# Turning the gates and the squares behind the quadrants of a decoder kernel, with another order of work in its first and last heads

## The chip, the cores and the metric

The kernel runs on one core of a Trainium2 chip. The metric is the device time of one execution in microseconds (us). Before the change the median of three runs is 1415.98 us, between 1415.79 and 1416.11.

## The reference, cut to what matters

The input is x, 16 sequences of 256 tokens with 512 features. Three blocks follow one another, each with a residual and a layer norm behind it: a gated state-space block, a long convolution that takes the place of cross attention, and a feed-forward block with low-rank experts. The change lies in the last two:

```python
# long convolution: D = 256 tokens are 32 heads x 8, L = 512
kv = vr[:, :, :, None, :] * x2r[:, :, None, :, :]
y = irfft(rfft(kv, n=1024) * k_f[None, :, None, None, :], n=1024)[..., :L]
y = y + kv * skip
out = jnp.einsum('bhijl,bhil->bhjl', y, x1r)
x = _layernorm(x + out)
# feed-forward with the two best of eight low-rank experts
base = x_flat @ W.T + b
logits = x_flat @ gate_w.T + gate_b
topk_logits, topk_idx = jax.lax.top_k(logits, 2)
gates = jax.nn.softmax(topk_logits, axis=-1)
xA = jnp.einsum('nd,erd->ner', x_flat, lora_A)
delta_all = jnp.einsum('ner,eor->neo', xA, lora_B)
...
out = base + lora_update
x = _layernorm(x + out)
```

## The kernel before, in words

All numbers are float32. Stage one (to about 760 us) is the state-space block; the change leaves it alone but for one constant. Stage two is one Python loop over the heads, `for h in range(HX)`, HX = 32; a head has 128 tokens (16 sequences by 8). The order of instructions on each engine is the order of the program, written out by hand (`manual_schedule`), so an instruction that waits holds up all that stands behind it on its engine.

Pass h of the loop convolves head h and does the feed-forward of head f = h - 1. It has two halves, one for each half q of the sequences.

- First half: four transposes turn v of the next head (`turned_v`, L147, tile `tr`); parts of earlier feed-forwards follow; then `turned_gates` (L1222) transposes `xa`, the gated low-rank activations of the head before, and ScalarE copies it to `xaT` (L1224). `seeded` (L1012) makes the seed product of the convolution, `spread_seed` lets ScalarE copy it into the other PSUM banks (L1019), and `convolve` makes four full products (L1030) and twelve 64x64 quadrant products (L1045). The last four quadrants wait for `one`, a tiny ScalarE copy (L1061) that itself waits for the first four.
- Second half: directly behind the quadrants `products_with_gates` multiplies the head's output `o_l` by the gate and low-rank weights `w_gl` (L1198: 8 gate columns, 128 low-rank columns and one column of 1/512 for the mean), and multiplies the squares `sq` by a column of 1/512 (L1202) for the mean square. Then come parts of the feed-forward, the seed and the convolution for q = 1.

A float32 product appears as two matmul records, a transpose as one.

VectorE contracts the convolution's result with the context: two products `pr` that read the PSUM banks of y (L1078) and two reductions `red` (L1088). It also makes the products `kv` of the next head (L157), and `gates` (L1119 to L1150), the ranking of the eight experts. GpSimd sums `ol` (L1402), folds the squares from 512 to 128 columns (L1190), takes the power -1/2 for the layer norm, and prepares `xs`, `Td` and `sk`. ScalarE makes the squares (L1186) and the mean squared (`m2`, L1207).

The feed-forwards of heads 1 to 30 go in pairs (`class Pair`), a seven-product scheme over 2x2 blocks with the products `first`, `second`, `third_and_fifth`, `sixth`, `fourth` and `seventh`, dealt over two passes. A pair begins in the second half of an odd pass (3, 5 and so on) with `first` and `third_and_fifth`. The even pass behind it makes `sixth` and `second` in its first half, and `fourth`, the first low-rank product and `finish` of the pair's first head in its second. `seventh`, the second low-rank product and the other `finish` (L1156, VectorE) follow in the first half of the next odd pass. All of a pair lies in two PSUM banks, `al` and `be`. Head 0 is alone: four plain products of 512 columns (`feed_forward`, L1238) and one low-rank product (`lora`) into one bank, `base`. Two of the four are made in pass 1, two and the low-rank product in pass 2. Head 31 is finished behind the loop, among the last full products of its own convolution: `convolve(..., True, steps=...)` calls one step ahead of each of them.

PSUM tiles of the tag `tr` (two buffers) hold `tr` and `gl` in turn; `gl` has the products of L1198 and L1202, then serves VectorE as scratch for the ranking (`room`), and takes the turned gates in its last 128 columns (`XAT`). The lines around the change:

```python
            if nxt:
                seed = seeded(y, T, xs, 1, h == 0)
            if ff:
                if f == 0:
                    feed_forward(base, o_l, (1,))
                    alone = base, o_l, rs
                elif second:
                    pair.third_and_fifth()
...
                turning = gates(gl, rs, gl[:, NG + 2 :]), gl[:, XAT]
            if nxt:
                convolve(y, kv, T, Td, 1)
```

Of the kernel before, what the change touches and what calls it, by code (L numbers as in the profile page):

```python
# [72 lines left out]
def decoder_kernel(  # L73
# [108 lines left out]
    with ExitStack() as s1:  # L182
# [370 lines left out]
        for g in range(groups):  # L553
# [339 lines left out]
            if g == 0:  # L893
                skip_bc = wp.tile([P, S], F32, name="skip_bc")
                nc.sync.dma_start(skip_bc, skip.partition_broadcast(P))
                w_gl = wp.tile([P, KD, NG + 1], F32, name="w_gl")
                nc.gpsimd.memset(w_gl[:, :, NG:], 1.0 / D)
# [12 lines left out]
                share = wp.tile([P, P], F32, name="share")  # L910
                nc.gpsimd.memset(share, 1.0 / D)
# [4 lines left out]
    with ExitStack() as s2:  # L916
# [197 lines left out]
            nc.gpsimd.tensor_tensor(rs, var, nhalf[:, 0:1], ALU.pow)  # L1114
            return nm, rs

        def gates(gl, rs, room):


            seen, rank = [room[:, 2 * NE * NE + n * NE :][:, 0:NE] for n in range(2)]  # L1120
            lg = p2.tile([P, NE], F32, tag="lg", name="lg")
            for to in (seen, lg):
# [27 lines left out]
            return xa  # L1150
# [40 lines left out]

            return sq[:, 0:P], folded

        def products_with_gates(o_l, sq):

            gl = ps_t.tile([P, D], F32, tag="tr", name="gl")
            for kc in range(KD):
                nc.tensor.matmul(  # L1198
                    gl[:, 0 : NG + 1], o_l[:, kc, :], w_gl[:, kc, :],
                    start=(kc == 0), stop=(kc == KD - 1),  # L1200
                )
            last = nc.tensor.matmul(  # L1202
                gl[:, NG + 1 : NG + 2], sq, share[:, 0:1],
                start=True, stop=True, skip_group_check=True,
            )
# [4 lines left out]
        def spread_of(gl, m2):  # L1210

            var = p2.tile([P, 1], F32, tag="var_b", name="var_b")
            nc.vector.scalar_tensor_tensor(
                var, gl[:, NG + 1 : NG + 2], LN_EPS, m2, ALU.add, ALU.subtract
            )
            rs = p2.tile([P, 1], F32, tag="rs_h", name="rs_h", bufs=4)
            nc.gpsimd.tensor_tensor(rs, var, nhalf[:, 0:1], ALU.pow)
            return rs

        def turned_gates(xa, room):  # L1220
            xat = room[0:ER, 0:P]
            nc.tensor.transpose(xat, xa.rearrange("p e r -> p (e r)"), ident)  # L1222
            xaT = p2.tile([ER, P], F32, tag="xaT", name="xaT")
            nc.scalar.copy(xaT, xat)  # L1224
            return xaT

        HD = D // 2
        LO, HI, ALL = slice(0, HD), slice(HD, D), slice(0, D)
        XAT = slice(D - P, D)

        def lora(ps, xaT, cols, start=False):
            nc.tensor.matmul(  # L1232
# [123 lines left out]
        last, alone, turning = None, None, None  # L1356
        pair, closing, ready = None, None, None
        for h in range(HX):
            nxt, ff, f = h + 1 < HX, last is not None, h - 1
# [8 lines left out]
            if h:  # L1368
# [4 lines left out]
                        vns.append(load_v(h + 2))  # L1373
                        cTs.append(load_c(h + 2))
                opened = pair if pair is not None and len(pair.o) == 2 else None
                if alone is not None:
                    feed_forward(alone[0], alone[1], (2, 3))
                if opened is not None:
                    opened.sixth()
                if closing is not None:  # L1380
                    closing.seventh()
                xaT = turned_gates(*turning) if turning is not None else None
                if pair is not None:
                    pair.xaT.append(xaT)
# [5 lines left out]
                if alone is not None:  # L1390
# [7 lines left out]
            if ff:  # L1398
# [7 lines left out]
                    ALU.add,  # L1406
                )
                sq, folded = squares(o_l)
                if alone is not None:
                    base, _, rs_f = alone  # L1410
                    ready = finish(0, ((ALL, base, b_bc),), rs_f, folded)
                    alone = None
# [36 lines left out]
            y = new_y()  # L1449
            o = with_residual(skip_term(cT, ws, behind), vT)  # L1450
            if ff:
                gl, m2 = products_with_gates(o_l, sq)
                if second:
                    pair.first()
                if closing is not None:
                    closing.fourth()
                    closing.scaled_first()
                if not nxt:
                    pair.sixth()
                rs = spread_of(gl, m2)  # L1460
                if second and nxt:
                    pair.sums_second()
                if f == 0:
                    base = ps_b.tile([P, D], F32, tag="al", name="base")
                    feed_forward(base, o_l, (0,), True)
            if nxt:
                seed = seeded(y, T, xs, 1, h == 0)
            if ff:
                if f == 0:
                    feed_forward(base, o_l, (1,))  # L1470
                    alone = base, o_l, rs
# [20 lines left out]
            if ff:  # L1492
                if second and nxt:
                    pair.sums_third()
                if not nxt:
                    pair.common()
                turning = gates(gl, rs, gl[:, NG + 2 :]), gl[:, XAT]
            if nxt:
                convolve(y, kv, T, Td, 1)
                if closing is not None:  # L1500
# [6 lines left out]


        o_f, red_f, y_f, cT_f = last
        o_l = {}  # L1510

        def contracted(src, ks):

# [42 lines left out]
            )  # L1556

        def turn():
            pair.xaT.append(turned_gates(*turning))
# [11 lines left out]
        convolve(  # L1571
            y_f, kv, T, Td, 1, True, steps=(pair.second, turn, pair.lora_of_first, rest)
        )
        tr = ps_t.tile([P, KD, P], F32, tag="tr", name="tr")
        base = ps_y.tile([P, 2, D], F32, tag="y0", name="y0")[:, 0, :]
# [94 lines left out]
```

## Time and profile before

| what | value |
|---|---|
| median of three runs | 1415.98 us |
| the profiled execution, its own time | 1415.68 us |
| its span, first to last instruction | 1413.9 us |
| TensorE (PE) matmul busy | 1397.6 us, 99% |
| VectorE (DVE) busy | 1179.5 us, 83% |
| GpSimd (POOL) busy | 612.4 us, 43% |
| ScalarE (ACT) busy | 422.3 us, 30% |
| mean granted clock of TensorE | 0.998 |

PE is the row of matmuls, PEld that of weight loads, which mostly run beside matmuls. Each matmul's record lasts longer than its turn in the array: what counts for the time is the distance from one start to the next. A row of a timeline has its start, its length, the engine, the line, the operation, and in brackets the idle time before it with what ended that. The chain of waits names the work that followed on itself without a gap and ended last.

### The profile page before, as it was taken

Reading aid. Unit: us, or ns where it says so; the run is one execution under the profiler, and the core shown is the slowest. Engines: PE = TensorE matmul, PEld = TensorE weight load, DVE = VectorE, ACT = ScalarE, POOL = GpSimd, SP = SyncE. Lnnn points to the kernel's source line nnn. Section 1 sums busy time; section 2 is a strip of 40 time slices with the busy share of each in tenths; the row PEclk is TensorE's granted clock in tenths of the full one; section 3 lists DMA queues with packets and bytes.
Section 4 is the critical chain, followed back from the end, with each engine's and each line's share of the span. In section 5 each row is a group of like instructions: output and inputs, shape, how many; then the busy total and the mean of one; then the engine's idle time right before and its main releaser. Section 6 shows DMA issues by size and latency. Waiting matters only on the chain.

```text
span 1413.9 us, 19593 instructions
## 1 busy us (share of the span) xinstructions
PE 1397.6 (99%) x7122; PEld 953.6 (67%) x7122; DVE 1179.5 (83%) x2270; ACT 422.3 (30%) x917; POOL 612.4 (43%) x816
## 2 busy tenths in 40 slices
PE   9999999999999999999999999999999999999997
PEld 7888888787888888878885355454545555555543
DVE  6988878878888787877857888898989888889886
ACT  2423323233232332332311323332323233333321
POOL 5450011110100201001005677788777777788774
PEclk9999999999999999999999999999999999999999
DMA  8013111120121111203003112221222122212200
GB/s 303 33 38 133 34 58 45 38 84 8 52 71 45 56 36 39 84 22 92 31 8 115 58 40 75 76 69 51 75 68 67 48 73 75 75 53 68 68 27 30
DMA packets 49168, 89.20 MB, mean 63 GB/s; under 512 B 8880, under 2 KB 13360, under 8 KB 49072
## 3 DMA queue, kind: packets, MB, share of 16 engines
q1 hardware_dynamic: 49072, 87.96, 19.6%
q8 instruction: 56, 0.92, 0.3%
q14 instruction: 40, 0.33, 0.1%
HBM read 70.62 MB, written 17.32 MB: 62 GB/s over the span
## 4 chain that ended last, share of the span: by engine, by line
PE 95%; DVE 2%; POOL 2%; issue 1%; DMA 0%; ACT 0%; SPq 0%; POOLq 0%; DVEq 0%
PE mm L330 21%; PE y L1030 15%; PE s L330 14%; PE y L1045 12%; PE s L782 6%; PE mm L782 6%; PE y L1012 4%; PE be L1260 4%; PE al L1260 3%; PE gl L1198 2%; PE tr L147 1%; PE xm L599 1%; PE mm L739 1%; PE mm L873 1%; PE al L1232 1%; PE s L873 1%
## 5 line engine op out<-in xcount | busy, mean ns | idle before, releaser
L1078 DVE TENSOR_TENSOR pr<-y,cT 128x1024 f32<-128x1024 f32 x126 | 148.4, 1219 | 59.1 <-PE y L1045 59.1
L1045 PE MATMUL y<-kv 64*64 64x512 f32 x1536 | 179.8, 598 | 0.6 <-ACT one L1061 0.6
L588 DVE SCALAR_TENSOR_TENSOR acc<-xi,wc,acc 128x512 f32<-128x512 f32 x192 | 142.0, 753 | 7.4 <-ACT acc L584 1.7
L1088 DVE TENSOR_REDUCE red<-pr 128x128 f32<-128x1024 f32 x126 | 147.1, 1209 | 0.0
L157 DVE TENSOR_TENSOR kv<-tr,cT 128x1024 f32<-128x1024 f32 x124 | 145.5, 1215 | 0.0
L1045 PEld LDWEIGHTS y<-kv 64*64 64x64 f32 x1536 | 52.2, 132 | 119.5 <-issue 96.6
L1030 PE MATMUL y<-kv 128*128 128x512 f32 x272 | 128.9, 595 | 2.0 <-DVE pr L1078 1.7
L68 POOL TENSOR_TENSOR rs_a<-ve_a,nhalf 128x1 f32<-128x1 f32 x32 | 19.0, 592 | 242.5 <-DVE ve_a L66 242.5
L391 POOL TENSOR_TENSOR rstd<-ms,nhalf 128x4 f32<-128x4 f32 (+1 forms) x9 | 8.5, 948 | 251.4 <-DVE ms L389 251.4
L1030 PE MATMUL y<-kv,Td 128*128 128x512 f32 x248 | 116.5, 592 | 0.0
L330 PE MATMUL mm<-XT,w_z 128*128 128x256 f32 x384 | 90.7, 379 | 0.0
L1030 PEld LDWEIGHTS y<-kv,Td 128*128 128x128 f32 x248 | 47.2, 190 | 59.2 <-issue 55.7
L1030 PEld LDWEIGHTS y<-kv 128*128 128x128 f32 x272 | 50.9, 190 | 43.6 <-ACT y L1019 18.5
L996 POOL TENSOR_TENSOR xs<-kv 128x512 f32<-128x512 f32 x63 | 80.2, 1272 | 0.1
L1019 ACT COPY y<-y 64x512 f32<-64x512 f32 x120 | 67.0, 558 | 44.2 <-PE y L1012 41.9
L330 PEld LDWEIGHTS mm<-XT,w_z 128*128 128x128 f32 x384 | 73.1, 190 | 9.8
L330 PE MATMUL mm<-xnT,w_z 128*128 128x256 f32 x288 | 70.8, 382 | 0.0
L1402 POOL TENSOR_TENSOR ol<-o,red 128x512 f32<-128x512 f32 x31 | 39.3, 1269 | 69.7 <-DVE red L1088 69.7
L223 POOL TENSOR_TENSOR XT<-xnT 128x512 f32<-128x512 f32 x7 | 9.2, 1310 | 129.0 <-PE mm L782 129.0
L1012 PE MATMUL y<-xs,kv 128*128 128x512 f32 x120 | 62.8, 605 | 0.8 <-POOL xs L996 0.7
L330 PE MATMUL s<-XT,w_xi 128*128 128x256 f32 x256 | 61.0, 380 | 0.8 <-DVE XT L226 0.5
L330 PEld LDWEIGHTS mm<-xnT,w_z 128*128 128x128 f32 x288 | 54.1, 190 | 10.0 <-issue 3.0
(326 smaller groups left out, 3053.6 us busy)
## 6 DMA issues: line engine op xcount, KB each, us to landing
cT<-in_ctxT SPq DMA_DIRECT2D x32, 384.0 KB
kv<-in_toep SPq DMA_DIRECT2D x32, 384.0 KB
xt<-in_x SPq DMA_DIRECT2D x32, 256.0 KB
spread<-both SPq DMA_DIRECT2D x32, 256.0 KB
first<-xt SPq DMA_DIRECT2D x32, 256.0 KB
vn<-first SPq DMA_DIRECT2D x32, 256.0 KB
out<-res SPq DMA_DIRECT2D x31, 256.0 KB
xnT<-in_xT SPq DMA_DIRECT2D x7, 1024.0 KB
```

The costliest lines, as they stand in the source:

```text
L157: last = nc.vector.tensor_tensor(kv[:, q, k * BQ : (k + NL // 2) * BQ], vT[:, q, blks].rearrange("p k (b i) -> p (k b) i", i=NH).unsqueeze ...
L330: nc.tensor.matmul(ps, w[:, p, a, kc, :], Xs[b][:, kc, :], start=start and kc == 0, stop=stop and kc == 1, skip_group_check=upon,)
L588: ins = nc.vector.scalar_tensor_tensor(acc, xi[:, :, k : k + S], wc[:, c, k : k + 1], acc, ALU.mult, ALU.add)
L782: nc.tensor.matmul(ps, own[a][c][:, n * P : (n + 1) * P], w_o[b][c], start=start and c == 0, stop=stop and c == HC - 1, skip_group_check=upon,
L996: return nc.gpsimd.tensor_tensor(xs[:, q], moving(kv, q, 0), moving(kv, q, 1), ALU.add)
L1012: nc.tensor.matmul(seed, T[:, SHARED_AT, :], xs[:, q], start=True, stop=True)
L1019: nc.scalar.copy(bank_of(y, 2)[b : b + HP], seed[a : a + HP])
L1030: nc.tensor.matmul(bank_of(y, lb), w, moving(kv, q, mb), start=not late and lb not in begun, stop=False, skip_group_check=True,)
L1045: return nc.tensor.matmul(bank_of(y, lb)[cols], T[rows, DIAGONAL_AT, (b - a) * HP : (b - a + 1) * HP], moving(kv, q, lb)[rows], start=star ...
L1078: nc.vector.tensor_tensor(pr.rearrange("p (k b j) i -> p k b j i", k=2, j=NH), y[i].rearrange("p k (b j i) -> p k b j i", j=NH, i=NH), cT[ ...
L1088: nc.vector.tensor_reduce(red[:, q, 2 * i : 2 * i + 2, :].rearrange("p k t -> p (k t)"), pr, AX.X, ALU.add)
L1260: nc.tensor.matmul(ps, a[:, kc, :], w[:, kc, :], start=(start and kc == 0), stop=(kc == 1), skip_group_check=True,)
```

## The change

- `products_with_gates` begins with two transposes directly behind the quadrants: that of `xa` of the head before (taken out of the first half, so it runs half a pass later), and that of `sq`. The product of `sq` by the column of 1/512 goes. `w_gl` gets one column more, of -1/512, so mean squared is the product of two of its columns.
- ScalarE sums the turned squares by an activation with `accum_out` (128x128 out of PSUM) in place of squaring the mean (128x1), and copies the turned gates (`turned_copy`) in the second half.
- Head 0's feed-forward: product 0 in pass 1 behind the seed, 1 and 2 in the first half of pass 2, 3 in its second half, the low-rank product and `finish` in pass 3.
- Last head: `sixth` behind `third_and_fifth`; the finishing of head 29 (`first_finished`) one step ahead of `seventh` and the second low-rank product, with a full product between them; the ranking of the very last head has its scratch in SBUF, and one scaled copy of the logits less.

```diff
-        def products_with_gates(o_l, sq):
+        def products_with_gates(o_l, sq, xa):
             gl = ps_t.tile([P, D], F32, tag="tr", name="gl")
+            if xa is not None:
+                nc.tensor.transpose(gl[0:ER, XAT], xa.rearrange("p e r -> p (e r)"), ident)
+            turned = gl[:, NG + 2 : NG + 2 + P]
+            nc.tensor.transpose(turned, sq, ident)
             for kc in range(KD):
                 nc.tensor.matmul(
-                    gl[:, 0 : NG + 1], o_l[:, kc, :], w_gl[:, kc, :],
-                    start=(kc == 0), stop=(kc == KD - 1),
+                    gl[:, 0 : NG + 2], o_l[:, kc, :], w_gl[:, kc, :],
+                    start=(kc == 0), stop=(kc == KD - 1), skip_group_check=True,
                 )
-            last = nc.tensor.matmul(
-                gl[:, NG + 1 : NG + 2], sq, share[:, 0:1],
-                start=True, stop=True, skip_group_check=True,
-            )
-            m2 = p2.tile([P, 1], F32, tag="m2", name="m2")
-            wait_for(nc.scalar.activation(m2, gl[:, NG : NG + 1], AF.Square), last)
-            return gl, m2
+            ms = p2.tile([P, 1], F32, tag="ms", name="ms")
+            nc.scalar.activation(
+                sq, turned, AF.Identity, bias=eps, scale=1.0 / D, accum_out=ms
+            )
+            return gl, ms
...
+        def turned_copy(room):
+            xaT = p2.tile([ER, P], F32, tag="xaT", name="xaT")
+            nc.scalar.copy(xaT, room[0:ER, 0:P])
+            return xaT
...
                 var, gl[:, NG + 1 : NG + 2], LN_EPS, m2, ALU.add, ALU.subtract    # before
+                var, gl[:, NG : NG + 1], gl[:, NG + 1 : NG + 2], ms, ALU.mult, ALU.add
...
-                if alone is not None:
-                    feed_forward(alone[0], alone[1], (2, 3))
+                if h == 2:
+                    feed_forward(base, alone, (1,))
+                if h == 3:
+                    lora(base, xaT, ALL)
...
-                xaT = turned_gates(*turning) if turning is not None else None
                 seed = seeded(y, T, xs, 0, h == 1)
...
-                    lora(alone[0], xaT, ALL)
+                if h == 2:
+                    feed_forward(base, alone, (2,))
...
-                gl, m2 = products_with_gates(o_l, sq)
+                gl, ms = products_with_gates(o_l, sq, xa)
+                if xa is not None:
+                    xaT = turned_copy(gl[:, XAT])
...
-                if not nxt:
-                    pair.sixth()
...
-                    feed_forward(base, o_l, (1,))
+                    feed_forward(base, o_l, (0,), True)
                 elif second:
                     pair.third_and_fifth()
+                    if not nxt:
+                        pair.sixth()
                 else:
                     pair = Pair(f, o_l)
+                if f == 1:
+                    feed_forward(base, alone, (3,))
...
-        def rest():
-            ready.append(pair.finish(0))
+        def first_finished():
+            ready.append(pair.finish(0))
+        def rest():
             pair.seventh()
             pair.lora_of_second()
...
-        xaT = turned_gates(gates(gl, rs, gl[:, NG:]), gl[:, XAT])
+        xaT = turned_gates(gates(gl, rs), gl[:, XAT])
```

More of the change, by code (lines that the diff above doesn't have):

```diff
@@ L895, in decoder_kernel @@
                 nc.sync.dma_start(skip_bc, skip.partition_broadcast(P))
-                w_gl = wp.tile([P, KD, NG + 1], F32, name="w_gl")
-                nc.gpsimd.memset(w_gl[:, :, NG:], 1.0 / D)
+                w_gl = wp.tile([P, KD, NG + 2], F32, name="w_gl")
+                for n, part in enumerate((1.0 / D, -1.0 / D)):
+                    nc.gpsimd.memset(w_gl[:, :, NG + n : NG + n + 1], part)
                 nc.sync.dma_start(w_gl[:, :, 0:NG], WglT.rearrange("(k p) e -> p k e", p=P))
@@ L1115, in centred_squares, with gates @@
             return nm, rs
-        def gates(gl, rs, room):
-            seen, rank = [room[:, 2 * NE * NE + n * NE :][:, 0:NE] for n in range(2)]
+        def gates(gl, rs, room=None):
             lg = p2.tile([P, NE], F32, tag="lg", name="lg")
-            for to in (seen, lg):
+            if room is None:
+                room = p2.tile([P, 2 * NE * NE + NE], F32, tag="cmp", name="cmp", bufs=1)
+                rank, seen = room[:, 2 * NE * NE :], lg
+            else:
+                seen, rank = [room[:, 2 * NE * NE + n * NE :][:, 0:NE] for n in range(2)]
+            for to in (lg,) if seen is lg else (seen, lg):
                 nc.vector.scalar_tensor_tensor(to, gl[:, 0:NE], rs, gb_bc, ALU.mult, ALU.add)
@@ L1192, in squares, with spread_of @@
             return sq[:, 0:P], folded
[L1194 removed]
+        HD = D // 2
+        LO, HI, ALL = slice(0, HD), slice(HD, D), slice(0, D)
+        XAT = slice(D - P, D)
+        eps = w2.tile([P, 1], F32, name="eps")
+        nc.gpsimd.memset(eps, LN_EPS / P)
+        def products_with_gates(o_l, sq, xa):
             gl = ps_t.tile([P, D], F32, tag="tr", name="gl")
+            if xa is not None:
+                nc.tensor.transpose(gl[0:ER, XAT], xa.rearrange("p e r -> p (e r)"), ident)
+            turned = gl[:, NG + 2 : NG + 2 + P]
+            nc.tensor.transpose(turned, sq, ident)
             for kc in range(KD):
                 nc.tensor.matmul(
[L1199 to L1210 removed]
+                    gl[:, 0 : NG + 2], o_l[:, kc, :], w_gl[:, kc, :],
+                    start=(kc == 0), stop=(kc == KD - 1), skip_group_check=True,
+                )
+            ms = p2.tile([P, 1], F32, tag="ms", name="ms")
+            nc.scalar.activation(
+                sq, turned, AF.Identity, bias=eps, scale=1.0 / D, accum_out=ms
+            )
+            return gl, ms
[3 more added lines that the diff above has]
+            return xaT
+        def spread_of(gl, ms):
             var = p2.tile([P, 1], F32, tag="var_b", name="var_b")
             nc.vector.scalar_tensor_tensor(
[L1214 removed]
+                var, gl[:, NG : NG + 1], gl[:, NG + 1 : NG + 2], ms, ALU.mult, ALU.add
             )
@@ L1220, in turned_gates @@
         def turned_gates(xa, room):
[L1221 to L1229, printed above, removed]
+            nc.tensor.transpose(room[0:ER, 0:P], xa.rearrange("p e r -> p (e r)"), ident)
+            return turned_copy(room)
         def lora(ps, xaT, cols, start=False):
@@ L1354, in finish @@
                 return finish(self.f + head, self.parts(head), self.rs[head], between)
-        last, alone, turning = None, None, None
+        last, xa = None, None
         pair, closing, ready = None, None, None
@@ L1381, in decoder_kernel @@
                     closing.seventh()
-                xaT = turned_gates(*turning) if turning is not None else None
-                if pair is not None:
-                    pair.xaT.append(xaT)
                 seed = seeded(y, T, xs, 0, h == 1)
@@ L1389, in decoder_kernel @@
                     ready = None
-                if alone is not None:
-                    lora(alone[0], xaT, ALL)
+                if h == 2:
+                    feed_forward(base, alone, (2,))
                 if opened is not None:
@@ L1408, in decoder_kernel @@
                 sq, folded = squares(o_l)
[L1409 to L1412, printed above, removed]
+                if h == 3:
+                    ready = finish(0, ((ALL, base, b_bc),), rs_alone, folded)
                 elif closing is not None:
@@ L1451, in decoder_kernel @@
             if ff:
-                gl, m2 = products_with_gates(o_l, sq)
+                gl, ms = products_with_gates(o_l, sq, xa)
+                if xa is not None:
+                    xaT = turned_copy(gl[:, XAT])
+                    for one in (pair, closing):
+                        if one is not None and one.f <= f - 1 <= one.f + 1:
+                            one.xaT.append(xaT)
                 if second:
@@ L1457, in decoder_kernel @@
                     closing.scaled_first()
[L1458 to L1460 removed]
+                rs = spread_of(gl, ms)
                 if second and nxt:
                     pair.sums_second()
[L1463 to L1465 removed]
             if nxt:
@@ L1469, in decoder_kernel @@
                 if f == 0:
-                    feed_forward(base, o_l, (1,))
-                    alone = base, o_l, rs
+                    base = ps_b.tile([P, D], F32, tag="al", name="base")
+                    feed_forward(base, o_l, (0,), True)
+                    alone, rs_alone = o_l, rs
                 elif second:
                     pair.third_and_fifth()
+                    if not nxt:
+                        pair.sixth()
                 else:
                     pair = Pair(f, o_l)
+                if f == 1:
+                    feed_forward(base, alone, (3,))
                 if f:
@@ L1496, in decoder_kernel @@
                     pair.common()
-                turning = gates(gl, rs, gl[:, NG + 2 :]), gl[:, XAT]
+                xa = gates(gl, rs, gl[:, NG + 2 :])
             if nxt:
@@ L1509, in decoder_kernel @@
         o_f, red_f, y_f, cT_f = last
-        o_l = {}
+        gl_f, o_l = gl, {}
         def contracted(src, ks):
@@ L1558, in turn @@
         def turn():
-            pair.xaT.append(turned_gates(*turning))
+            pair.xaT.append(turned_gates(xa, gl_f[:, XAT]))
             pair.fourth()
@@ L1571, in decoder_kernel @@
         convolve(
-            y_f, kv, T, Td, 1, True, steps=(pair.second, turn, pair.lora_of_first, rest)
+            y_f, kv, T, Td, 1, True,
+            steps=(pair.second, turn, pair.lora_of_first, first_finished, rest),
         )
```

## The prediction

> **What bounds the kernel now.** I read the page's engine and chain rows, then the chain over two passes in mid-loop, then each place where TensorE's queue is held: its weight loads against VectorE's timeline, the early passes, the last one.
>
> ```profile
> PE 1397.6 (99%) x7122; PEld 953.6 (67%) x7122; DVE 1179.5 (83%) x2270; ACT 422.3 (30%) x917; POOL 612.4 (43%) x816
> PE 95%; DVE 2%; POOL 2%; issue 1%; DMA 0%; ACT 0%; SPq 0%; POOLq 0%; DVEq 0%
> ```
> ```profile
> 1019.95 0.11 PE gl L1202 x2
> 1020.06 0.97 PE al L1260 x4
> ...
> 1029.79 0.59 PE tr L147 x4
> 1030.37 0.87 PE al L1260 x4
> ```
> ```profile
> 1030.86 0.14 PEld L1222 LDWEIGHTS gl<-ident,xa 128*128 128x128 f32 x1
> 1031.11 0.30 PEld L1012 LDWEIGHTS y<-xs,kv 128*128 128x128 f32 x2
> ```
> ```profile
> 1029.82 2.36 DVE L1078 TENSOR_TENSOR pr<-y,cT 128x1024 f32<-128x1024 f32 x2 [1.56 <-PE y L1045]
> ```
> ```profile
> 1039.31 2.36 DVE L1078 TENSOR_TENSOR pr<-y,cT 128x1024 f32<-128x1024 f32 x2 [0.79 <-PE y L1045]
> 1041.58 2.33 DVE L1088 TENSOR_REDUCE red<-pr 128x128 f32<-128x1024 f32 x2
> 1043.83 0.15 DVE L1213 SCALAR_TENSOR_TENSOR var_b<-gl,m 128x1 f32<-128x1 f32 x1
> ...
> 1049.45 1.22 DVE L1078 TENSOR_TENSOR pr<-y,cT 128x1024 f32<-128x1024 f32 x1
> ```
> ```profile
> 779.30:799.70 20.40, 20.40 (x97) 8.77 (x93) 17.19 (x27) 6.55 (x14) 12.61 (x17) 1.00 0.18 52
> 799.70:818.30 18.60, 17.58 (x87) 6.72 (x83) 16.42 (x25) 5.07 (x12) 10.96 (x13) 1.00 0.22 71
> ```
> ```profile
> 1382.36 1.10 PE L1260 MATMUL al<-Tw,S 128*128 128x256 f32 x4 [0.55 <-ACT u L1296]
> 1387.71 0.66 PE L1045 MATMUL y<-kv 64*64 64x512 f32 x4 [0.65 <-ACT one L1061]
> 1394.50 1.13 PE L1260 MATMUL be<-Tw,ol 128*128 128x256 f32 x4 [0.22 <-DVE x L1156]
> ```
>
> TensorE looks like the only bound: 99% busy, 95% of the chain, every pair of passes 40.09 us. But its busy time hides waits of a tenth. The seed's weights load at 1031.11, 0.25 behind the load before instead of the 0.22 of one product's turn: VectorE's first `pr` began at 1029.82, lasts 1.22, ends at 1031.04, and frees the bank that the seed writes. And from `pr` to `pr` of an even pass's second half VectorE has no gap: 1039.31 to 1049.45, 10.14 us, where TensorE takes 10.12 from L1198 to the turned v. Two engines share the bound. In the table of early passes TensorE has 17.58 of work in 18.60.
>
> **The change part by part.** Distances are from start to start, instruction by instruction from the timeline.
>
> *The gate block, every second half.* Before: 0.519 from the last quadrant to L1198, 0.222 to its second record (a weight load that isn't hidden), 0.708 for six more, 0.115 and 0.027 for L1202, 0.112 to the next product, 0.299 to its second record: 2.002. (The same product L1260 costs 0.97 behind L1202 and 0.87 elsewhere.) After, by turned v, which stands behind quadrants already: 0.520, 0.165 to the second transpose, 0.110 to L1198, eight records of 0.118 are 0.945 (one column more is 0.8 ns), an ordinary 0.216: 1.956. Saved 0.046.
>
> *A rule against this.* The Trainium skill, "TensorE: Matmul & The Clock Gate", part 4, puts a transpose at about 275 ns in a kernel. Here one lasts 272 ns, but the next starts 0.109 later. By the rule the block would be 2.23, 0.23 dearer than before, and the sum below +4 in place of -1.8. I take the row.
>
> *The gates' transpose leaves the first half.* It costs 0.109, and the seed's second record 0.466 instead of 0.428: 0.147 if nothing else held the seed. But `pr` does. Without L1222 the load waits for the same `pr` and comes at the same 1.401 behind the turned v; a load that waits shows 0.534 to the second record (as where TensorE waits in the early passes), so that record stays at 1.936, where it is now. Gain 0, in even passes. In odd ones likewise, where `pr` itself starts when VectorE is done.
>
> *Even second halves.* TensorE's 0.046 doesn't count: VectorE's 10.14 does. And there the change adds: the variance's operation takes its scalar from PSUM instead of a constant. VectorE's spacing of such an operation over 256 columns is 0.331 with a constant (L821) and 0.400 with a scalar column (L1156): +0.07. Its bounds are 0 and 0.1; I take 0.07.
>
> *Odd second halves.* VectorE idles 1.56 behind it: 0.046 gained. Per pair then -0.046 + 0.07, by 14 pairs: +0.3.
>
> *What else could be late.* The squares: the second fold on GpSimd ends 1.07 us before L1198 in odd passes, 1.36 in even ones; their transpose starts 0.15 later than that. `xa` is ready half a pass early. ScalarE: the sum is nearest to the copy L1224 plus an accumulator read, 0.27 + 0.19 against 0.17, and `xaT` moves in (0.27): 0.56 more per second half. It idles 0.80 before `u` in odd passes and 1.66 before the seed copies in even ones, and VectorE takes up the variance only 4.63 behind L1198; if that cover went, the seed copies would hold the second full product. Turned squares and products share a bank; the skill's "PSUM — Partial Sum Buffer", bank collisions, says to guard by bank, and the 0.55 for `u` is such a wait. Written behind the products, the sum waits for them, not they for it: 0 on the path. The constants are memsets of 0.1 on an idle GpSimd.
>
> *The early passes.* A half without feed-forward is held by the two `pr`, the seed behind them, and its copies: 0.87 of waits in pass 2's second half, 1.58 in pass 3's first. After: pass 1's second half loses a product (0.857), its seed waits for `pr` at 1.38 behind the block's start with its reload: -0.64. Pass 2's first half loses the low-rank product and the transpose (1.0) and waits 0.2: -0.81. Pass 2's second half takes product 3 into its waits: +0.21. Pass 3's first takes the low-rank product into them, and VectorE and the seed copies set its end: -0.08. Sum -1.3. `finish` of head 0 (VectorE 0.83, ScalarE 0.9, GpSimd 1.2) comes one pass later, where VectorE idles 1.8 before `pr`; so does its store on the SP queue, which then stands between two passes' loads as every later head's does.
>
> *The last pass.* `sixth` no longer waits for `u`: 0.84 earlier at the quadrants. But `one` stands in ScalarE's queue behind the exponential, that behind the ranking and GpSimd's power, which follows its sums and `o` without a gap from 1379.4 on. None of that moves, so TensorE waits 0.84 longer: 0. Behind it `seventh` no longer waits for `finish`: 0.387 and 0.107 for a reload, 0.49. At the end one scaled copy of the logits less is 0.27 (1402.96 to 1403.23). The scratch in SBUF is bounded by 0 and 0.2; 64-column operations take 0.21 to 0.23 in either memory, so 0.01. Together 0.77.
>
> Sum: +0.3 - 1.3 - 0.8 = -1.8. From 1415.68, the profiled execution, 1413.9; the median lies 0.3 above it: 1414.2.
>
> **Rivals.** *VectorE doesn't hold the even halves* (0.17): the scalar costs nothing and `pr` starts with the quadrants' end. Then 27 halves x 0.046 = 1.2 in place of +0.3: 1412.7. For it: `pr` comes only 0.12 behind the turned v, 0.107 where nothing holds it. Against: no gap in its 10.14.
>
> *The seed isn't held* (0.08): all first halves gain 0.147, 27 x 0.193 = 5.2 in all, 1408.7. For it: the chain gives it to TensorE. Against: the load at 1031.11.
>
> *Slower: transposes at the rule's price* (0.08). Odd halves lose 0.23, even ones 10.35 against 10.14; 14 x 0.44 = +6.2, less 2.1: 1420.1. It decides from about 0.1 a block. For it: two more engines' semaphores stand directly behind the quadrants, and their loads aren't hidden. Against: 0.59 for four of turned v.
>
> *The ends are worth less* (0.09): if the early waits only move on, as in the last pass, 0.8 - 0.3 is left: 1415.5.
>
> The main case has 0.58.
>
> **How the numbers follow.** The main case's own range is 1413.0 to 1415.4 (early 0.9 to 1.8, pairs -0.6 to +0.7, last 0.5 to 1.0). The range 1411.8 to 1416.0 takes in the first rival and the small ends, and leaves out the two far ones. The measurement can tell about 0.2%, 2.8 us, from no change: faster has the first two rivals and the main case's lower edge, 0.33; slower 0.09; same 0.58.
>
> **What would show it.** L1202 gone, two transposes behind the quadrants, L1198's second record 0.118 behind its first; yet the pair of passes still 40.0 to 40.2, the seed's load still 1.40 behind the turned v, and VectorE gapless in even second halves with 0.13 from the variance to `kv` instead of 0.065. From pass 1's to pass 2's gate block 19.0 instead of 20.4, from 2 to 3 18.7. The wait for `one` at 1.5 and more in the last pass, none for `x` at `seventh`. Wrong if the pair takes 39.7 (the seed is free) or over 40.3 (transposes or ScalarE).

## The result, and the profile after

The changed kernel takes 1413.58 us, the median of 20 runs (1413.16 to 1414.79); beside it the kernel before took 1416.1. The ratio is 0.9984, with a 95% interval of 0.9977 to 0.9990: a gain of 2.5 us, small and measurable. The two profiled executions are 1415.68 and 1413.62, their spans 1413.9 and 1411.8: 2.1 apart, with a granted clock of 0.998 in both. The forecast was 1.8 less than the profiled execution of before.

The page of the kernel after, its engine row and its chain row:

```profile
PE 1396.9 (99%) x7091; PEld 949.5 (67%) x7091; DVE 1178.7 (83%) x2269; ACT 429.2 (30%) x948; POOL 612.9 (43%) x818
PE 95%; DVE 2%; issue 1%; DMA 1%; POOL 0%; ACT 0%; SPq 0%; POOLq 0%; DVEq 0%; ACTq 0%
```

They say almost nothing: 31 matmuls fewer, PE's busy time 0.7 us lower, the same 99% and 95%. What happened is in the starts. The chain over two passes in mid-loop, kernel after (start, length, what):

```profile
1017.72 0.26 PE gl L1209
1017.98 0.11 PE gl L1211
1018.09 0.95 PE gl L1213 x8
1019.03 0.86 PE al L1271 x4
...
1028.65 0.59 PE tr L147 x4
1029.24 0.86 PE al L1271 x4
1030.11 1.00 PE y L1013 x2
```

L1209 turns the gates, L1211 the squares, L1213 is the gate product. The separate product for the squares is gone, and with it the 0.11 that the following `al` product took longer (0.97 before, 0.86 now). Between the turned v and the seed only `al` is left; the transpose that was there before saved nothing by leaving, because the seed's load is held, as the next two views show. The weight loads, kernel after (in brackets the idle time before):

```profile
1028.58 0.42 PEld L147 LDWEIGHTS tr<-ident,vn 128*128 128x128 f32 x4 [0.81 <-issue]
1028.97 0.73 PEld L1271 LDWEIGHTS al<-Tw,S 128*128 128x128 f32 x4
1029.98 0.30 PEld L1013 LDWEIGHTS y<-xs,kv 128*128 128x128 f32 x2 [0.28 <-issue]
```

The seed's load comes 1.40 behind the turned v, with an idle 0.28 that the profile books as "issue". VectorE's timeline of the same stretch names the cause, and shows the even second half:

```profile
1028.69 2.36 DVE L1079 TENSOR_TENSOR pr<-y,cT 128x1024 f32<-128x1024 f32 x2 [1.46 <-PE y L1046]
...
1038.18 2.36 DVE L1079 TENSOR_TENSOR pr<-y,cT 128x1024 f32<-128x1024 f32 x2 [0.79 <-PE y L1046]
1040.45 2.34 DVE L1089 TENSOR_REDUCE red<-pr 128x128 f32<-128x1024 f32 x2
1042.70 0.21 DVE L1231 SCALAR_TENSOR_TENSOR var_b<-gl,ms 128x1 f32<-128x1 f32 x1
1042.83 2.35 DVE L157 TENSOR_TENSOR kv<-tr,cT 128x1024 f32<-128x1024 f32 x2
...
1048.37 2.35 DVE L1079 TENSOR_TENSOR pr<-y,cT 128x1024 f32<-128x1024 f32 x2
```

The first of the two `pr` starts at 1028.69, lasts 1.22, and ends at 1029.91; the seed's load follows at 1029.98. In the even half VectorE still has no gap, and its 10.14 have become 10.19: from the variance to `kv` 0.130 instead of 0.065.

TensorE's busy time in the two early stretches between the gate blocks of passes 1, 2 and 3, and its longer waits in the last pass:

```profile
779.44:798.39 18.95, 18.84 (x91) 7.79 (x87) 16.57 (x25) 5.76 (x12) 11.74 (x14) 1.00 0.18 56
798.39:817.13 18.74, 18.61 (x90) 7.36 (x86) 17.25 (x27) 5.34 (x14) 10.64 (x16) 1.00 0.18 57
```
```profile
1386.78 1.09 PE L1046 MATMUL y<-kv 64*64 64x512 f32 x8 [1.49 <-ACT one L1062]
...
1403.61 0.33 PE L1239 MATMUL gl<-ident,xa 128*128 128x128 f32 x1 [0.83 <-DVE xa L1147]
```

The last of these waits in the kernel before:

```profile
1405.59 0.33 PE L1222 MATMUL gl<-ident,xa 128*128 128x128 f32 x1 [1.38 <-DVE xa L1142]
```

The stretches were 20.40 and 18.60, with 20.40 and 17.58 of work. The second is 0.14 longer now, and all but full. In the last pass the waits for `u` (0.55) and for `x` (0.22) are gone, the one for `one` has grown from 0.65 to 1.49, and the one for the last ranking's `xa` has shrunk from 1.38 to 0.83.

The account, from one turned v to another in both traces: passes 1 to 4 lose 1.34 us (0.64, 0.60 and 0.10), a pair of passes goes from 40.086 to 40.101, and from the turned v of the last pass to the end 63.50 become 62.39. Together 1.34 + 1.11, less some 0.2 for the pairs, less 0.13 that stage one happened to take longer: 2.1.

### The profile page after: what moved, and what is told of

The parts are those of the page before. It is cut to its first block, busy times and chain, and to the rows that moved or that the text cites. A ratio compares the mean times of both kernels' runs of the same rounds, so it can differ in the third digit from the quotient of the medians.

```text
span 1411.8 us, 19609 instructions
## 1 busy us (share of the span) xinstructions
PE 1396.9 (99%) x7091; PEld 949.5 (67%) x7091; DVE 1178.7 (83%) x2269; ACT 429.2 (30%) x948; POOL 612.9 (43%) x818
## 4 chain that ended last, share of the span: by engine, by line
PE 95%; DVE 2%; issue 1%; DMA 1%; POOL 0%; ACT 0%; SPq 0%; POOLq 0%; DVEq 0%; ACTq 0%
PE mm L330 21%; PE y L1031 15%; PE s L330 14%; PE y L1046 12%; PE s L782 6%; PE mm L782 6%; PE y L1013 4%; PE be L1271 4%; PE al L1271 3%; PE gl L1213 2%; PE tr L147 1%; PE xm L599 1%; PE mm L739 1%; PE mm L873 1%; PE al L1243 1%; PE s L873 1%
```

## The experiments

Twelve kernels ran, in three groups of four. The kernel before had medians of 1416.02, 1416.09 and 1415.81 beside them. Stage one's end moves by up to 1.7 us between profiled executions (the turned v of pass 1 starts between 770.17 and 771.89), so the distances inside a trace say more than the totals.

**1. Only head 0's dealing.** Before, with product 0 in pass 1, 1 and 2 in the first half of pass 2, 3 in its second, the low-rank product and `finish` in pass 3.

```diff
-                if alone is not None:
-                    feed_forward(alone[0], alone[1], (2, 3))
+                if h == 2:
+                    feed_forward(base, alone, (1,))
+                if h == 3:
+                    lora(base, xaT_alone, ALL)
...
-                    lora(alone[0], xaT, ALL)
+                if h == 2:
+                    feed_forward(base, alone, (2,))
...
+                if f == 1:
+                    feed_forward(base, alone, (3,))
```

> The kernel before with one part of the change: head 0's feed-forward dealt over passes 1 to 3 as in the changed kernel, everything else as before (the gates' transpose stays in the first half, its low-rank input for head 0 is kept for pass 3). Theory (the dealt products fill waits that the two pr and the seed's copies make in passes 2 and 3): 1.1 to 1.3 us less than before, all of it between the turned v of pass 1 and that of pass 4, later passes at 40.09 a pair. Rival (the waits only move on to the next pass that is short of TensorE work): within 0.3 us of before.

1414.80 us, ratio 0.9992 (0.9984 to 1.0): 1.2 less, with an interval that reaches no change, so the starts in the trace have to decide. The turned v of passes 1 to 4 starts at 770.56, 788.91, 807.86 and 828.11, where the whole change has 770.56, 788.91, 807.86 and 828.07. So the dealing alone makes the early gain, and the pair keeps its 40.08.

**2. Only the last head.** Before, with the last head in the new order and its scratch in SBUF.

```diff
-                if not nxt:
-                    pair.sixth()
...
                     pair.third_and_fifth()
+                    if not nxt:
+                        pair.sixth()
...
-        def rest():
-            ready.append(pair.finish(0))
+        def first_finished():
+            ready.append(pair.finish(0))
+        def rest():
...
-        xaT = turned_gates(gates(gl, rs, gl[:, NG:]), gl[:, XAT])
+        xaT = turned_gates(gates(gl, rs), gl[:, XAT])
```

> The kernel before with the last head's part alone: sixth behind third_and_fifth, first_finished a step ahead of seventh, the last ranking in SBUF with one scaled copy less. Theory: 1.0 us less: 0.49 where seventh waited for finish, 0.55 in the last ranking; the earlier sixth gives nothing, since the wait of the quadrants for one grows from 0.65 to about 1.4. Rival (the earlier sixth counts as well): 1.8 us less, wait for one unchanged.

1414.86 us, ratio 0.9992 (0.9983 to 1.0). From the last pass's turned v to the end 62.46 in place of 63.50: 1.04. With the 1.3 of experiment 1 (from the turned v of pass 1 to that of pass 4) that makes 2.3, as much as the whole change gained inside its trace (2.24, stage one apart): what it does behind the quadrants of every pass added nothing. TensorE's row in this kernel shows that `sixth`'s 0.8 only moved into the wait for `one`, as forecast:

```profile
1387.79 1.09 PE L1045 MATMUL y<-kv 64*64 64x512 f32 x8 [1.44 <-ACT one L1061]
```

**3. A spare transpose in the first half.** After, with the gates' transpose made once more ahead of the seed.

```diff
                     closing.seventh()
+                if xa is not None:
+                    nc.tensor.transpose(gl[0:ER, XAT], xa.rearrange("p e r -> p (e r)"), ident)
                 seed = seeded(y, T, xs, 0, h == 1)
```

> The changed kernel with the gates' transpose made once more, where it stood before: ahead of the seed in every first half; its result is not read. Theory (the seed waits for the first pr anyway): free, pair of passes 40.1 as in the changed kernel, time within 0.3 us of it. Rival (TensorE alone bounds the loop): 0.147 in each of 29 first halves, pair 40.4, 4 us more than the changed kernel.

1413.55 us, ratio 0.9981 (0.9974 to 0.9989); pair 40.100, seed load 1.399 (even) and 1.520 (odd) behind the turned v, all as after. The seed is held by `pr`; a transpose in front of it is free.

**4. A spare transpose in the gate block.** After, with the squares turned twice.

```diff
             nc.tensor.transpose(turned, sq, ident)
+            nc.tensor.transpose(turned, sq, ident)
```

> The changed kernel with the transpose of the squares made twice behind the quadrants, to the same place. Theory (TensorE bounds odd second halves, VectorE the even ones with 10.21 against 10.08): 0.11 in odd passes only, pair 40.21, 1.5 us more than the changed kernel. Rival 1 (TensorE alone): 0.11 in all second halves, pair 40.32, 3.1 us more. Rival 2 (a transpose behind quadrants costs the 275 ns of the rule): over 0.27 in each, pair 40.5, 6 us more.

1415.23 us, ratio 0.9994 (0.9986 to 1.0002): 1.65 more than after, of which 14 pairs at 0.111 make 1.55. TensorE, this kernel, the block and the product behind it:

```profile
1019.52 0.33 PE L1209 MATMUL gl<-ident,xa 128*128 128x128 f32 x1
1019.69 0.27 PE L1211 MATMUL gl<-ident,sq 128*128 128x128 f32 x1
1019.80 0.27 PE L1212 MATMUL gl<-ident,sq 128*128 128x128 f32 x1
1019.91 1.11 PE L1214 MATMUL gl<-w_gl,ol 128*128 128x138 f32 x8
```

A queued transpose costs 0.11 here, though its record lasts 0.27. The pair grew by 0.111, not by twice that: the odd half pays, the even one doesn't, because the seed behind it waited for VectorE anyway (its load moves from 1.521 to 1.412 behind the turned v).

**5. The variance from a constant again.** After, with mean squared made by ScalarE, so that VectorE's operation has a constant and no scalar out of PSUM.

```diff
-            return gl, ms
+            m2 = p2.tile([P, 1], F32, tag="m2", name="m2")
+            nc.scalar.activation(m2, gl[:, NG : NG + 1], AF.Square)
+            return gl, (ms, m2)
...
-                var, gl[:, NG : NG + 1], gl[:, NG + 1 : NG + 2], ms, ALU.mult, ALU.add
+            nc.vector.scalar_tensor_tensor(var, ms[0], 0.0, ms[1], ALU.add, ALU.subtract)
```

> The changed kernel, but ScalarE also squares the mean (0.17, in its idle time), and VectorE's variance takes a constant in place of a scalar column out of PSUM. Theory (VectorE bounds even second halves, and the scalar column costs it 0.065): pair 40.04 instead of 40.105, 0.9 us less than the changed kernel. Rival (VectorE's chain is no bound): pair unchanged, time within 0.2 us.

1412.95 us, ratio 0.9977 (0.9968 to 0.9986); pair 40.046, 0.055 less than after. VectorE's rows, this kernel, the same place as above:

```profile
1042.59 0.15 DVE L1233 SCALAR_TENSOR_TENSOR var_b<-ms,m 128x1 f32<-128x1 f32 x1
1042.65 2.35 DVE L157 TENSOR_TENSOR kv<-tr,cT 128x1024 f32<-128x1024 f32 x2
```

The 0.065 came from VectorE's scalar, and nearly all of it counts. Whether a scalar column in SBUF would cost as much was not run. The medians differ by 0.63 where 14 pairs make 0.77.

**6. The variance on GpSimd.** As 5, with the operation off VectorE altogether.

```diff
-            nc.vector.scalar_tensor_tensor(
-                var, gl[:, NG : NG + 1], gl[:, NG + 1 : NG + 2], ms, ALU.mult, ALU.add
-            )
+            nc.gpsimd.tensor_tensor(var, ms[0], ms[1], ALU.subtract)
```

> The changed kernel, but ScalarE also squares the mean, and GpSimd takes the difference of both for the variance: VectorE has one operation less in each second half. Theory: VectorE's even half falls by 0.13 from 10.21 to 10.08 and meets TensorE's 10.08: pair 39.97, 1.9 us less than the changed kernel. Rival (TensorE alone): unchanged. Rival (GpSimd's queue, 93% busy in that half, takes over): pair 40.2 or more.

1412.41 us, ratio 0.9972 (0.9961 to 0.9983). The pair is 39.980, as the theory had it, and the odd seed's load is back at 1.399: VectorE no longer ends last there. The total gained 1.17 and not 1.9. Inside the trace the loop gains 1.59 (from the turned v of pass 4 to that of the last pass 519.75 instead of 521.34), and the last pass loses 0.2 (62.59 to its end instead of 62.39; it has one more GpSimd operation ahead of the power). That leaves 1.4; the medians' 1.17 differs from it by less than this kernel's runs do (1411.57 to 1413.41).

**7. Every ranking in SBUF.** After, with the scratch that helped the last head given to all.

```diff
-                xa = gates(gl, rs, gl[:, NG + 2 :])
+                xa = gates(gl, rs)
```

> The changed kernel with the ranking of all heads as the last head has it: scratch in SBUF, one scaled copy of the logits less. In the last head it took 0.55 less on VectorE. Theory: even second halves are then bounded by TensorE, 0.13 less: pair 39.97, 1.9 us less than the changed kernel, the remaining 0.4 of VectorE's gain unused. Rival (VectorE and GpSimd get in each other's way in SBUF, which the scratch in PSUM avoids): the ranking's operations or GpSimd's grow, and the pair stays at 40.1 or goes above.

1449.14 us, ratio 1.0232 (1.0218 to 1.0246): 36 us slower than after. The theory of a gain fell, and the rival of a clash with GpSimd was right; it had named no size. VectorE and GpSimd, this kernel, the same three microseconds:

```profile
1060.00 0.21 DVE L1137 TENSOR_TENSOR cmp<-lg 128x64 f32<-128x64 f32 x1
1060.13 1.52 DVE L1138 TENSOR_TENSOR cmp<-lg 128x64 f32<-128x64 f32 x1
1061.58 1.30 DVE L1139 TENSOR_TENSOR cmp<-cmp,tri 128x64 f32<-128x64 f32 x1
```
```profile
1060.02 1.54 POOL L933 TENSOR_TENSOR sk<-kv,skip_bc 128x512 f32<-128x512 f32 x1
1061.52 1.27 POOL L997 TENSOR_TENSOR xs<-kv 128x512 f32<-128x512 f32 x1
```

The second comparison, 0.23 long in PSUM, lasts here as long as the GpSimd operation beside it: it ends 0.09 behind `sk`, and the masking behind it ends 0.09 behind `xs`. From 850 to 1345 us all 47 held ones end 0.08 to 0.09 behind a GpSimd operation. The first comparison starts as GpSimd goes over from one operation to the next, and isn't held (0.232 at the longest). GpSimd loses next to nothing (`sk` 1.508 at the median against 1.484). The Trainium skill, "SBUF — State Buffer", "Who interferes with whom", has the rule: a VectorE operation with both inputs in SBUF contends with a GpSimd operation that reads SBUF; the section "SBUF: two separate sides" adds that whichever starts first keeps the port for its whole length, and the other is blocked. This trace agrees. The pages give no time; here the second comparison and the masking take up to 1.52 us, the gated exponential (`ex`) up to 0.74, and the pair takes 42.25. The trace of the kernel before had one such case: of eight sums `ol` of 128x64 in its last pass (L1537, both inputs in SBUF) seven last 0.21 to 0.23, and one 0.748, until 0.08 behind GpSimd's `ub`.

**8. Three reliefs at once.** 6 and 7 and, beside them, the gates' transpose back in the first half.

> The changed kernel with both bounds relieved at their places: the gates' transpose back in the first half, where the seed waits anyway; variance on GpSimd and ranking in SBUF. Theory: the block without the second transpose takes 0.11 less in both second halves: pair 39.97 - 0.22 = 39.75, about 5 us less than the changed kernel (1408.6). Rival (TensorE alone): first halves 0.147 more, second 0.11 less: pair 40.18, 1 us more than the changed kernel.

1449.93 us, ratio 1.0239 (1.0225 to 1.0253); pair 42.500. It has 7's clash in it and says nothing of its own question, which 9 asks again without it.

**9. The gates' transpose back in the first half, the variance on GpSimd.** The ranking stays in PSUM, and the last head keeps VectorE's variance.

```diff
-        def products_with_gates(o_l, sq, xa):
+        def products_with_gates(o_l, sq):
             gl = ps_t.tile([P, D], F32, tag="tr", name="gl")
-            if xa is not None:
-                nc.tensor.transpose(gl[0:ER, XAT], xa.rearrange("p e r -> p (e r)"), ident)
...
+            if nxt:
+                nc.gpsimd.tensor_tensor(var, ms[0], ms[1], ALU.subtract)
...
                     closing.seventh()
+                if xa is not None:
+                    xaT = turned_gates(xa, gl[:, XAT])
```

> The changed kernel with the gates' transpose back in the first half, and the variance of heads 0 to 29 as in pool_var (ScalarE squares the mean, GpSimd subtracts); the ranking keeps its scratch in PSUM, and the last pass its variance on VectorE. Theory (the seed waits for pr in any case, so the transpose is free there; it costs 0.11 only behind the quadrants): odd second halves 0.11 less than in pool_var, even ones held by VectorE at 10.08: pair 39.87, and the last pass 0.2 less than pool_var: 3.2 us less than the changed kernel, 1410.3. Rival (TensorE alone bounds the loop): the first halves lose 0.147 and the second gain 0.11: pair 40.05 and 1413.5.

1410.15 us, ratio 0.9961 (0.9948 to 0.9975); pair 39.867. Against 6 the pair loses 0.113, one transpose. The weight loads, this kernel, the stretch shown above:

```profile
1026.89 0.42 PEld L147 LDWEIGHTS tr<-ident,vn 128*128 128x128 f32 x4 [0.81 <-issue]
1028.04 0.14 PEld L1242 LDWEIGHTS gl<-ident,xa 128*128 128x128 f32 x1
1028.29 0.30 PEld L1013 LDWEIGHTS y<-xs,kv 128*128 128x128 f32 x2
```

The transpose (L1242) stands again between the turned v and the seed, and the seed's load comes 1.40 behind the turned v as ever: it lies inside the wait for `pr`.

**10. `one` ahead of the exponential.** After, with head 30's ranking issued behind the last pass's quadrants, so that ScalarE reaches `one` before it reaches `ex`.

```diff
-                xa = gates(gl, rs, gl[:, NG + 2 :])
+                if nxt:
+                    xa = gates(gl, rs, gl[:, NG + 2 :])
...
+        def opening():
+            nonlocal xa
+            xa = gates(gl_f, rs_31, gl_f[:, NG + 2 :])
+            pair.second()
...
-            steps=(pair.second, turn, pair.lora_of_first, first_finished, rest),
+            steps=(opening, turn, pair.lora_of_first, first_finished, rest),
```

> The changed kernel with one thing else in the last pass: the ranking of head 30 is issued behind the quadrants, so that one no longer stands behind the exponential in ScalarE's queue. Theory (that queue holds TensorE 1.5 us there): the wait for one goes, the next wait is that of the turned gates for the ranking, and 1.0 to 1.3 us are gained at the end. Rival (VectorE's contraction sets the end anyway): within 0.3 us of the changed kernel, the wait reappearing in front of the turned gates.

1412.65 us, ratio 0.9978 (0.9969 to 0.9987): 0.93 less than after. ScalarE's queue around `one` in the kernel after, then in this one, then this one's products:

```profile
1386.35 0.30 ACT L1132 ACTIVATE ex<-lg,nm 128x8 f32<-128x8 f32 x1 [4.41 <-DVE nm L1130]
1386.56 0.17 ACT L1062 COPY one<-nhalf 128x1 f32<-128x1 f32 x1
```
```profile
1384.56 0.19 ACT L1062 COPY one<-nhalf 128x1 f32<-128x1 f32 x1 [2.55 <-PE y L1046]
```
```profile
1383.40 2.81 PE L1046 MATMUL y<-kv 64*64 64x512 f32 x24
...
1387.10 1.02 PE L1031 MATMUL y<-kv 128*128 128x512 f32 x2
1388.32 0.33 PE L1239 MATMUL gl<-ident,xa 128*128 128x128 f32 x1 [0.20 <-DVE xa L1147]
```

The 1.49 is gone from the quadrants. Some 0.4 of it comes back at the turned gates, which now wait for the late `xa` (1.22 from the product before instead of 0.86), and 0.2 at the product (`be`) behind the following full products (1.93 instead of 1.72).

**11. 9 and 10 together.**

> gates_back and one_first together, as the version that should be fastest: 1409.2 if both theories hold, 1410.3 if only the first, 1412.5 if only the second.

1409.70 us (1408.69 to 1409.91), ratio 0.9954 (0.9942 to 0.9967): the fastest here, 6.1 less than the kernel before and 3.9 less than the change. Against 9 the median gains only 0.45, but inside the profiled execution the last pass takes 61.23 against 62.25, the full 1.0; its stage one ended 0.8 later than in 9's.

**12. Only one input of the comparisons in SBUF.** After, with the scratch in SBUF but one of the two scaled copies of the logits left in PSUM.

```diff
-                seen, rank = [room[:, 2 * NE * NE + n * NE :][:, 0:NE] for n in range(2)]
+                seen = room[:, 2 * NE * NE :][:, 0:NE]
+                room = p2.tile([P, 2 * NE * NE + NE], F32, tag="cmp", name="cmp", bufs=1)
+                rank = room[:, 2 * NE * NE :]
```

> The changed kernel with half of sbuf_rank: the ranking's scratch in SBUF, but one copy of the logits still in PSUM, so that the two comparisons have one input in SBUF and one in PSUM, while the masking (scratch and tri) and the last product (rank and ex) have both in SBUF. Theory (an operation of VectorE with both inputs in SBUF waits until GpSimd's operation is over, one with a single input there does not): the comparisons stay at 0.22, the masking takes 1.0 to 1.5 and ex 0.45 as in sbuf_rank; even second halves are 1 us or more longer, 12 us or more in all. Rival (any use of SBUF beside GpSimd is slow): the comparisons take 0.7 to 1.5 too.

1431.48 us, ratio 1.0111 (1.0097 to 1.0125); pair 41.23. The operations on the scratch, this kernel (shortest, median and longest in ns):

```profile
L1139 DVE TENSOR_TENSOR cmp<-gl,lg x24: 214/214/216, 867.9 to 1341.9; 128x64 f32<-128x64 f32 x24
L1140 DVE TENSOR_TENSOR cmp<-gl,lg x24: 214/215/216, 868.1 to 1342.0; 128x64 f32<-128x64 f32 x24
L1141 DVE TENSOR_TENSOR cmp<-cmp,tri x24: 332/698/1072, 868.2 to 1342.1; 128x64 f32<-128x64 f32 x24
L1144 DVE SCALAR_TENSOR_TENSOR ex<-cmp,ex x24: 733/846/955, 869.0 to 1343.6; 128x8 f32<-128x8 f32 x24
```

The comparisons, with one input in PSUM, are never held, 216 at the longest, though in each of these passes GpSimd's `Td` or `sk` runs beside them. The masking and the gated exponential, with both in SBUF, are held every time. That settles 7: it is the second SBUF input, not the place of the output. VectorE, this kernel, one of these rankings:

```profile
1032.84 0.21 DVE L1139 TENSOR_TENSOR cmp<-gl,lg 128x64 f32<-128x64 f32 x1
1032.97 0.21 DVE L1140 TENSOR_TENSOR cmp<-gl,lg 128x64 f32<-128x64 f32 x1
1033.10 0.34 DVE L1141 TENSOR_TENSOR cmp<-cmp,tri 128x64 f32<-128x64 f32 x1
```

From one start to the next it is 0.13 here, with an input in PSUM and the output in SBUF, where the ranking that also writes PSUM takes 0.26.

## Why the prediction was right

It said 1414.2, and the measurement is 1413.58; by its own reckoning from the profiled execution, -1.8 against -2.1. The chance of 0.58 stood on "within 0.2%", and the ratio of 0.9984 is inside that, its interval reaching beyond on the faster side.

- *The gate block*: forecast 1.956, measured 1.955 (0.520, 0.164, 0.109, eight records 0.948, 0.214). The 0.109 from a transpose's start to the next held; the about 275 ns of the Trainium skill, "TensorE: Matmul & The Clock Gate", part 4, are the length of a record here (0.273), not its price. Experiment 4 measured the price, 0.111, and the rival of dear transposes falls.
- *The seed is held by `pr`*: right, by the loads at 1.399, by experiments 3 and 9, and by 6, where an earlier `pr` lets the odd seed go earlier. The rival of a free seed falls.
- *Pairs*: +0.02 forecast, +0.015 measured. The 0.046 of TensorE counts in odd halves and VectorE's 0.065 in even ones; the rival that VectorE doesn't hold the even halves (39.99 a pair) falls with 5 and 6.
- *Early passes*: -0.64, -0.60 (0.81 less 0.21) and -0.13 (0.08, with 0.046 of pass 3's block) forecast, -0.64, -0.60 and -0.10 measured; experiment 1 has them alone, and 2 the last pass. The rival "the ends are worth less" falls.
- *Last pass*: forecast 0 for `sixth` (the wait for `one` grew by 0.84), 0.49 for `seventh` (0.490: from 11.393 to 10.903 between the third quadrant group and the last contraction), 0.27 for one scaled copy less. The last ranking gained 0.55.

**The step that was mis-sized** is the scratch in SBUF: "bounded by 0 and 0.2 ... so 0.01". It gained 0.28, beyond its own upper bound. The prediction compared the lengths of single operations, which differ little (about 0.22 in SBUF, 0.22 to 0.23 in PSUM). What counts is the distance of one start from the next. In the kernel before the comparisons and the masking of this last ranking are followed at 0.256, 0.267 and 0.266, in the kernel after at 0.133, 0.134 and 0.255: 0.27 in all. VectorE, the last ranking, kernel before and kernel after:

```profile
1403.57 0.22 DVE L1132 TENSOR_TENSOR gl<-gl,lg 128x64 f32<-128x64 f32 x1
1403.83 0.23 DVE L1133 TENSOR_TENSOR gl<-gl,lg 128x64 f32<-128x64 f32 x1
1404.10 0.23 DVE L1134 TENSOR_TENSOR gl<-gl,tri 128x64 f32<-128x64 f32 x1
```
```profile
1401.88 0.22 DVE L1137 TENSOR_TENSOR cmp<-lg 128x64 f32<-128x64 f32 x1
1402.01 0.22 DVE L1138 TENSOR_TENSOR cmp<-lg 128x64 f32<-128x64 f32 x1
1402.15 0.22 DVE L1139 TENSOR_TENSOR cmp<-cmp,tri 128x64 f32<-128x64 f32 x1
1402.40 0.29 DVE L1140 TENSOR_REDUCE cmp<-cmp 128x8 f32<-128x128 f32 x1
```

An input in PSUM alone doesn't cost this: in experiment 12 a comparison reads PSUM and writes SBUF, and the next starts 0.13 later. Leaving out the 0.13 by which stage one happened to end later, the change gained 2.24 inside the trace, 0.4 more than forecast: 0.27 is this term, and the pairs' smaller loss (0.2 instead of 0.3) is most of the rest. That the totals lie only 0.3 apart is in part the luck of stage one. The medians' 2.5 is 0.4 more than the 2.1 of the two profiled executions, which is no more than the spread of runs.

What the forecast had in its sums and didn't conclude is that moving the gates' transpose is a loss: it gave nothing by leaving the first half, and behind the quadrants it costs 0.11 in every odd half. So the two edits that apply to all passes gave next to nothing: the block's net gain of 0.046 in odd halves is lost again in even ones, where the variance's new scalar costs 0.065. Putting the transpose back and taking the variance off VectorE (experiment 9) gains 3.4 us on the change, more than all of the change gained.

## What to carry to other kernels

Where two engines share a bound, each hides what the other gains: find the half in which each ends last, and count an edit only there (0.11 a pair for a transpose in both halves, not 0.22). A place in front of a load that waits for another engine is free as long as the wait covers it; work moved out of it is worth nothing, and costs where it goes. Before scratch moves from PSUM to SBUF, see which operations then have both inputs in SBUF, and whether GpSimd reads SBUF beside them: the same move gained 0.28 us once, at the end with GpSimd idle, and cost 36 us in the loop.

## What the runs showed of the hardware that was not expected

- A 64-column VectorE operation with both inputs in SBUF lasts up to 1.52 us, in place of 0.22, beside a GpSimd operation that reads SBUF, and ends with it; with one input in PSUM it stays at 0.214 to 0.216 (experiments 7 and 12).
- Behind a 64-column VectorE comparison that writes PSUM the next start comes 0.26 to 0.27 later, behind one that writes SBUF 0.13, with GpSimd idle (the last ranking) or at work and one input in PSUM (experiment 12).
